# Layer norm, time attention, band attention and feed-forward: scores of two groups in one block, and rstd on other engines

## The chip, the cores and the metric

The kernel runs on one core of a Trainium2 chip. A core has five engines that run at the same time and wait for each other by semaphores: TensorE (PE in the profile; PEld is its weight load), VectorE (DVE), ScalarE (ACT), GpSimd (POOL) and SyncE (SP), which here only issues DMA. Matrix products are written to PSUM, which has 8 banks of 512 float32 values in each of 128 partitions[...]. All data is float32. The metric is the device time in microseconds (us) of one execution.

## The reference, cut to what matters

The input `x` has the shape (B, T, FB, C) = (2, 256, 128, 128). Three residual blocks follow each other: attention over time with a causal mask, attention over bands with a mask of width 16, and a feed-forward block.

```python
def _ln(x, w, b, eps=1e-05):
    mu = x.mean(-1, keepdims=True)
    var = ((x - mu) ** 2).mean(-1, keepdims=True)
    return (x - mu) * jax.lax.rsqrt(var + eps) * w + b

def _mha(x, wi, bi, wo, bo, h, mask):
    c = x.shape[-1]; dh = c // h
    q, k, v = jnp.split(x @ wi.T + bi, 3, axis=-1)
    split = lambda t: t.reshape(t.shape[:-1] + (h, dh)).swapaxes(-2, -3)
    q, k, v = (split(q), split(k), split(v))
    scores = jnp.einsum('...hqd,...hkd->...hqk', q, k) * (1.0 / np.sqrt(dh)) + mask
    o = jnp.einsum('...hqk,...hkd->...hqd', softmax(scores), v)
    return o.swapaxes(-2, -3).reshape(x.shape) @ wo.T + bo

xt = _ln(x, ln_t_w, ln_t_b).transpose(0, 2, 1, 3)
x = x + _mha(xt, t_wi, t_bi, t_wo, t_bo, 4, causal).transpose(0, 2, 1, 3)   # over time, 256 steps
x = x + _mha(_ln(x, ln_f_w, ln_f_b), f_wi, f_bi, f_wo, f_bo, 4, band16)     # over 128 bands
h = gelu(_ln(x, ln_n_w, ln_n_b) @ w1.T + b1)                                # 128 -> 512
x = x + (h @ w2.T + b2)
```

With 256 time steps and tiles of 128 keys, the causal mask leaves, for each head and sequence, the first key tile against both query tiles (256 columns) and the second key tile against the second query tile (128 columns). The two diagonal blocks are cut by a triangle.

## The kernel before, in words

Weights, biases and norm scales are folded beforehand (`fold`). The work is cut into groups of NT = 4 tiles of 128 tokens. First come 128 groups of time attention (`OverTime`; a group is two sequences `s` of 256 steps), which write an intermediate to device memory. Then, for each of 16 runs of 32 time steps, come 8 groups of band attention (`OverBands`) and 8 groups of the feed-forward block (`FeedForward`). I call the first part the time stage.

`BoundedPath.run` is a pipeline written out by hand. One turn of its loop, here called a step, does different stages of several neighbouring groups: scores of group n, the weighted sum of group n - 1, the projections of n + 1, normalizing of n + 3, statistics of n + 4. `do(n, ...)` calls the named stages of a group if it exists, `do_at` only if it is of the named class. All engine instructions go through `InOrder`, so each engine runs them in exactly the order in which the loop calls them; that is why the profile gives the one line 848 (the helper) for nearly all instructions, and why groups are told by tiles. A wait at the head of an engine's queue holds up everything behind it.

The stages of a time group, by the names of their tiles:

- `statistics`: mean and variance (`stats`, then `mv`) by DVE. `root`: rstd = (var + eps) to the power -0.5, by two POOL instructions on 128x4 values (`rstd`).
- `normalize`: four DVE instructions write `xh`. `turn`: DVE transposes 32x32 blocks (`z`) and four DMAs write it to device memory (`turned`). `fetch`: a DMA reads it back transposed (`xnT`).
- `queries_keys`, `values`: products `qp`, `kp`, `vp`, copied by ACT to `qT`, `kT`, `v`. Where the group ahead is attention, `product` splits the weights into four pieces of 32 columns, which stand beside each other in the array.
- scores, `first_half` and `second_half`, one for each sequence: for each of 4 heads a product of 256 columns and one of 128, both with a contraction of 32 rows, so the four heads stand in four row strips of the array. They fill four banks `sp` of 384 columns. ACT takes the exponentials, one instruction a head (`pt<-sp`, 128x384). POOL masks the two diagonal blocks of the four heads (two selects of 128x512), and the sum of the two key tiles' weights for the second queries is formed by POOL for one sequence and by DVE for the other (`pt<-pt`, 128x512).
- `weigh`: weights times values (`op`, contraction of 128, 32 columns a head) and the row sums (`rp`). `invert`: ACT forms 1/rp as exp(-ln(rp)). `divide`: DVE forms `t` and `u` (each with one input in PSUM) and from both `oT`.
- `output`, `finish`: the product `yp`, and DVE adds it to `res`, where POOL (`bias`, `res<-x,orow`) has put x plus a bias row.

PSUM banks come from one pool of 8 buffers, in turn. Lines of code that the change leaves as they are but that matter for it:

```python
vector.scalar_tensor_tensor(self.oT, t, 2.0, u, ALU.subtract, ALU.mult)          # both inputs in SBUF
engine.tensor_tensor(self.block(s, 3), self.block(s, 1), self.block(s, 2), ALU.add)   # both in SBUF
```

Of the kernel before, what the change touches and what calls it, by code (L numbers as in the profile page):

```python
# [19 lines left out]
P = 128  # L20
H = 4
# [414 lines left out]
class Group:  # L436
# [27 lines left out]
    def root(self):  # L464
# [2 lines left out]
        gpsimd.tensor_scalar(self.rstd, self.mv[:, :, 1], EPS, None, ALU.add)  # L467
        gpsimd.tensor_tensor(self.rstd, self.rstd, path.k.mhalf, ALU.pow)

    def normalize(self):  # L470
        path, vector = self.path, self.path.vector
        self.xh = path.work.tile([P, NT, P], F32, name="xh", bufs=2)
        for i in range(NT):
            vector.tensor_scalar(
                self.xh[:, i, :], self.src()[:, i, :], self.mv[:, i, 0:1], self.rstd[:, i : i + 1],
                ALU.subtract, ALU.mult,
            )
# [18 lines left out]
    def first_half(self):  # L496
        pass
# [13 lines left out]
    def second_mask(self):  # L511
        pass

    def last_sum(self):
        pass

    def queries_keys(self):
        pass

# [27 lines left out]

class Attention(Group):
    which = None

    def bias(self):
        self.path.gpsimd.tensor_tensor(
# [3 lines left out]
    def queries_keys(self):  # L556
        path = self.path
        wf = path.k.wf[self.which]
        self.qp = path.bank([P, NT * P], "qp")
        product(path, self.qp, wf[:, 0:P], self.xnT)  # L560

        self.kp = path.bank([P, NT * P], "kp")
        product(path, self.kp, wf[:, P : 2 * P], self.xnT)

    def take_query(self):
# [9 lines left out]
    def values(self):  # L575
        path = self.path
        wv = path.k.wf[self.which][:, 2 * P : 3 * P]
        self.vp = path.bank([P, NT, P], "vp")
        for i in range(NT):
            product(path, self.vp[:, i], self.xnT[:, i * P : (i + 1) * P], wv)  # L580

    def take_values(self):
        path = self.path
        self.v = path.work.tile([P, NT, P], F32, name="v")
        path.scalar.copy(self.v, self.vp)

    def invert(self):
# [27 lines left out]

    def output(self):
        path = self.path
        self.yp = path.bank([P, NT, P], "yp")
        for i in range(NT):
            product(path, self.yp[:, i], self.oT[:, i * P : (i + 1) * P], path.k.wn[self.which])  # L620

# [6 lines left out]
def rows_of(h):  # L628
    return slice(h * D, (h + 1) * D)
# [11 lines left out]
class OverTime(Attention):  # L641

    which = 0
    W = 3 * P

    def scores(self, s):
        path = self.path  # L650
        W, a = self.W, 2 * s * P
        self.sp = [path.bank([P, W], "sp") for h in range(H)]
        for h in range(H):
            r = rows_of(h)
            path.tensor.matmul(
                self.sp[h][:, 0 : 2 * P], self.kT[r, a : a + P], self.qT[r, a : a + 2 * P], start=True, stop=True
            )
        for h in range(H):
            r = rows_of(h)
            path.tensor.matmul(  # L660
                self.sp[h][:, 2 * P : W], self.kT[r, a + P : a + 2 * P], self.qT[r, a + P : a + 2 * P],
                start=True, stop=True,
            )

    def weights(self, s):
        path = self.path
        for h in range(H):
            path.scalar.activation(self.p[:, s, h, 0 : self.W], self.sp[h], AF.Exp)

    def mask(self, s):  # L670
        path = self.path
        for n in (2, 0):
            blk = self.block(s, n)
            path.gpsimd.affine_select(
                out=blk, in_=blk, compare_op=ALU.is_ge, fill=path.zero, base=0,
                pattern=[[0, H], [1, P]], channel_multiplier=-1,
            )

    def block(self, s, n):
        return self.p[:, s, :, n * P : (n + 1) * P]  # L680

    def add(self, engine, s):
        engine.tensor_tensor(self.block(s, 3), self.block(s, 1), self.block(s, 2), ALU.add)

    def first_half(self):
        self.p = self.path.work.tile([P, 2, H, self.W + P], F32, name="pt", tag="p", bufs=2)
        self.scores(0)

    def first_function(self):
        self.weights(0)  # L690

    def first_mask(self):
        self.mask(0)
        self.add(self.path.gpsimd, 0)

    def second_half(self):
        self.scores(1)

    def second_function(self):
        self.weights(1)  # L700

    def second_mask(self):
        self.mask(1)

    def last_sum(self):
        self.add(self.path.vector, 1)

    def weigh_one(self, op, s):
        path, p, v, W = self.path, self.p, self.v, self.W
        for h in range(H):  # L710
            r = rows_of(h)
            path.tensor.matmul(op[r, s, :], v[:, 2 * s, r], p[:, s, h, 0 : 2 * P], start=True, stop=False)
        for h in range(H):
            r = rows_of(h)
            path.tensor.matmul(
                op[r, s, P : 2 * P], v[:, 2 * s + 1, r], p[:, s, h, 2 * P : W], start=False, stop=True
            )

    def weigh(self):
        path = self.path  # L720
        op = path.bank([P, 2, 2 * P], "op")
        rp = path.bank([P, 2, 2 * P], "rp")
        self.weigh_one(op, 0)
        sums = self.p.rearrange("p s h (n q) -> p s h n q", q=P)[:, :, :, 0:4:3, :]
        for h in range(H):
            path.tensor.matmul(rp[rows_of(h), :, :], path.k.ones[:, 0:D], sums[:, :, h], start=True, stop=True)
        self.weigh_one(op, 1)
        self.op = op.rearrange("p s q -> p (s q)")
        self.rp = rp.rearrange("p s q -> p (s q)")


class OverBands(Attention):
# [32 lines left out]
            path.vector.tensor_tensor(blk, blk, path.band.unsqueeze(1).to_broadcast([P, NT, P]), ALU.mult)  # L765

    def first_half(self):
        self.p = self.path.work.tile([P, H, NT, P], F32, name="pf", tag="p", bufs=2)
        self.scores(range(H))

    def weigh(self):
# [15 lines left out]
class FeedForward(Group):  # L787
# [20 lines left out]

    def first_half(self):
        self.hp = {}  # L810
        self.hT = self.path.work.tile([P, self.path.k.NI, NT * P], F32, name="hT")
        self.hidden((0, 1))

    def first_function(self):
# [38 lines left out]
class BoundedPath:  # L853
    def __init__(self, ctx, tc, k):
# [1 line left out]
        self.xpool = ctx.enter_context(tc.tile_pool(name="xpool", bufs=3))  # L856
        self.work = ctx.enter_context(tc.tile_pool(name="work", bufs=3))
        self.small = ctx.enter_context(tc.tile_pool(name="small", bufs=6))
        self.ps = ctx.enter_context(tc.tile_pool(name="ps", bufs=8, space=PSUM))
        self.tensor, self.vector = InOrder(tc, tc.nc.tensor), InOrder(tc, tc.nc.vector)  # L860
        self.scalar, self.gpsimd = InOrder(tc, tc.nc.scalar), InOrder(tc, tc.nc.gpsimd)
        self.dram = ctx.enter_context(tc.tile_pool(name="turns", bufs=3, space=DRAM))
        self.zero = 0.0
        once = ctx.enter_context(tc.tile_pool(name="once", bufs=1))

        self.band = once.tile([P, P], F32, name="band")
        tc.nc.gpsimd.memset(self.band, 1.0)
# [3 lines left out]
                pattern=[[-s, P]], channel_multiplier=s,  # L871
            )

    def bank(self, shape, name):
        return self.ps.tile(shape, F32, name=name, tag="ps")

    @staticmethod
    def of_times(ap, i, f):
# [78 lines left out]
    def run(self, x, out):  # L957
# [17 lines left out]
        for n in range(-11, len(groups) + 2):  # L975
            feeds = [at(n - 2 + i, FeedForward) for i in range(5)]
            bands = [at(n - 2 + i, OverBands) for i in range(5)]
            turn = feeds[2] and bands[1]
            self.by_columns = at(n - 1, Attention)
            do(n + 11, "load")  # L980
            do_at(n + 4, OverTime, "statistics")
            if bands[2] and feeds[1]:
                self.scalar.preload_act_table_set(EXP_SET)
            do(n, "first_half", "first_function", "first_mask")
            if turn:
                do(n, "second_half", "second_function")
            do_at(n + 2, Attention, "fetch")
            do_at(n + 1, FeedForward, "fetch")
            do_at(n + 2, FeedForward, "normalize", "turn")
            do_at(n + 3, Attention, "normalize", "turn")  # L990
            do_at(n + 3, FeedForward, "statistics", "root")
            do_at(n + 4, OverTime, "root")
            if bands[2]:
                do(n, "second_mask")
            do(n - 1, "weigh")
            do(n - 1, "invert_exactly" if turn else "invert")
            if bands[2] or turn:
                do(n - 2, "output", "finish")
            do(n - 1, "divide")
            if not turn:  # L1000
                do(n, "second_half", "second_function")
            if not bands[2]:
                do(n, "second_mask", "bias")
                do_at(n + A, OverBands, "bias")
                if at(n - 1, FeedForward) and at(n - 2, OverBands):
                    do_at(n + A - 1, OverBands, "statistics", "root")
                if not turn:
                    do_at(n + A, OverBands, "statistics", "root")
            do(n + 1, "queries_keys", "take_query", "take_key")
            if not bands[2] and not turn:  # L1010
                do(n - 2, "output", "finish")
            do(n + 1, "values", "take_values")
            do(n, "last_sum")


def bounded_path(tc, k, x, out):
# [66 lines left out]
```

## Time and profile before

| | |
|---|---|
| time, median of 3 | 2792.8 us (2791.96 to 2794.28) |
| busy: PE, DVE, ACT, POOL | 98%, 82%, 65%, 74% of the span |
| time stage | up to about 1030 us |
| DMA | 343.70 MB, mean 123 GB/s |

A row of the timeline gives the start, how long it lasts in us, the engine, the line, the operation, the tiles written and read, the shape and the count of instructions merged into it; in brackets stands how long the engine sat idle before it, and what ended the wait. Matrix products overlap in the array, so the starts of consecutive blocks tell more about what PE needs than their lengths. A row of busy time by windows gives the window, its length, and for PE, PEld, DVE, ACT and POOL the busy us with the number of instructions, then the granted clock of TensorE, the DMA share and the rate.

### The profile page before, as it was taken

How to read it: one execution, taken by the hardware profiler on the slowest of the kernel's cores; microseconds unless marked ns; L12 is line 12 of the kernel's file. 1: busy time of each engine (PE TensorE's matmuls, PEld its weight loads, DVE VectorE, ACT ScalarE, POOL GpSimd, SP SyncE). 2: the span in 40 equal slices, each digit the busy share in tenths (PEclk: the TensorE clock that was granted, in tenths of full speed). 3: DMA queues.
4: the chain of work that ended last, by engine and by line, in shares of the span. 5: the costliest groups of instructions: out<-in, count | busy, mean ns of one | idle time of the engine just before them, and what ended most of it. 6: DMA issues, size and time to landing. Idle time of an engine off the chain costs nothing.

```text
span 2791.8 us, 103916 instructions
## 1 busy us (share of the span) xinstructions
PE 2733.2 (98%) x42534; PEld 1844.4 (66%) x42534; DVE 2302.8 (82%) x6446; ACT 1800.7 (65%) x3328; POOL 2062.7 (74%) x2569
## 2 busy tenths in 40 slices
PE   4999999999999989999999999999999999999998
PEld 3666666666666656676776766767766667667666
DVE  5888888888888899788787797797887887977975
ACT  2888888788888866646546556456466475564563
POOL 3899999999999996666676676676666766766762
PEclk9999999999999999999999999999999999999999
DMA  5555555545555554543544534535435345444333
GB/s 119 134 148 136 139 139 142 145 131 151 133 142 142 140 137 111 131 123 99 140 102 112 132 104 123 129 96 130 127 100 136 104 108 130 103 125 115 83 99 85
DMA packets 471301, 343.70 MB, mean 123 GB/s; under 512 B 43296, under 2 KB 405152, under 8 KB 470816
## 3 DMA queue, kind: packets, MB, share of 16 engines
q1 hardware_dynamic: 469568, 335.92, 46.5%
q8 instruction: 337, 5.52, 0.8%
q14 instruction: 148, 1.21, 0.1%
q10 hardware_dynamic: 1248, 1.05, 0.1%
HBM read 169.03 MB, written 167.77 MB: 121 GB/s over the span
## 4 chain that ended last, share of the span: by engine, by line
PE 89%; DVE 4%; DMA 3%; POOL 3%; SPq 1%; issue 1%; ACT 0%; DVEq 0%; POOLq 0%
PE zp L848 16%; PE hp L848 15%; PE sp L848 12%; PE op L848 9%; PE qp L848 8%; PE rp L848 7%; PE vp L848 7%; PE kp L848 7%; PE yp L848 7%; DMA xnT<-turned 1%; DVE xh L848 1%; POOL pf L848 1%; DMA turned<-z 1%; POOL rstd L848 1%; POOL pt L848 1%
## 5 line engine op out<-in xcount | busy, mean ns | idle before, releaser
L848 POOL TENSOR_SCALAR_AFFINE_SELECT pf<-pf 128x512 f32<-128x512 f32 x768 | 520.9, 694 | 270.6 <-ACT pf L848 244.3
L848 ACT ACTIVATE hT<-hp,b 128x512 f32<-128x512 f32 x512 | 349.3, 687 | 548.6 <-PE hp L848 539.1
L848 DVE TENSOR_SCALAR xh<-x,mv,rstd 128x128 f32<-128x128 f32 x1536 | 624.0, 467 | 17.4 <-POOL rstd L848 17.4
L848 PEld LDWEIGHTS zp<-w2T_sb,hT 128*128 128x128 f32 x4096 | 476.3, 192 | 56.2 <-issue 54.0
L848 PE MATMUL zp<-w2T_sb,hT 128*128 128x128 f32 x4096 | 479.8, 275 | 0.1
L848 PE MATMUL hp<-xnT,w1f 128*128 128x512 f32 x1024 | 470.5, 596 | 6.7 <-DMA xnT<-turned 5.5
L848 POOL TENSOR_TENSOR rstd<-rstd,mhalf 128x4 f32<-128x4 f32 x384 | 446.9, 1164 | 32.0
L848 ACT ACTIVATE pt<-sp 128x384 f32<-128x384 f32 x1024 | 419.5, 497 | 58.8 <-PE sp L848 58.5
L848 PE MATMUL sp<-qT,kT 32*128 32x128 f32 (+1 forms) x8192 | 397.0, 316 | 0.9 <-ACT kT L848 0.8
L848 POOL TENSOR_SCALAR_AFFINE_SELECT pt<-pt 128x512 f32<-128x512 f32 x512 | 323.0, 652 | 79.6 <-ACT pt L848 79.6
L848 PEld LDWEIGHTS sp<-qT,kT 32*128 32x128 f32 x8192 | 315.3, 185 | 83.1 <-issue 31.4
L848 DVE BATCH_NORM_STATS2 stats<-x 128x6 f32<-128x128 f32 x1536 | 326.5, 273 | 7.7 <-DMA x<-in_x 7.7
L848 POOL TENSOR_SCALAR rstd<-mv 128x4 f32<-128x4 f32 x384 | 88.6, 231 | 298.7 <-DVE mv L848 297.5
L848 ACT ACTIVATE pf<-sp 128x512 f32<-128x512 f32 x512 | 264.3, 603 | 62.4 <-PE sp L848 59.1
L848 PEld LDWEIGHTS hp<-xnT,w1f 128*128 128x128 f32 x1024 | 181.1, 190 | 184.6 <-issue 107.9
L848 PE MATMUL qp<-xnT,wf 128*32 128x512 f32 (+1 forms) x1856 | 270.6, 600 | 26.1 <-DMA xnT<-turned 26.1
L848 PEld LDWEIGHTS yp<-wn,oT 128*32 128x32 f32 (+1 forms) x7808 | 234.1, 111 | 83.8 <-issue 61.8
L848 DVE STREAM_TRANSPOSE z<-xh 128x512 f32<-128x512 f32 x384 | 273.2, 712 | 18.8 <-DMA turned<-z 5.7
L848 PEld LDWEIGHTS vp<-wf,xnT 128*32 128x32 f32 (+1 forms) x7424 | 237.3, 113 | 75.0 <-issue 65.5
L848 PE MATMUL vp<-wf,xnT 128*32 128x128 f32 (+1 forms) x7424 | 271.9, 273 | 0.5 <-DVE t L848 0.5
L848 PE MATMUL yp<-wn,oT 128*32 128x128 f32 (+1 forms) x7808 | 271.1, 273 | 0.3 <-DVE t L848 0.3
L848 DVE TENSOR_TENSOR pf<-pf,band 128x512 f32<-128x512 f32 x128 | 117.4, 917 | 184.8 <-ACT pf L848 177.3
(90 smaller groups left out, 3974.0 us busy)
## 6 DMA issues: line engine op xcount, KB each, us to landing
turned<-z SPq DMA_DIRECT2D x1536, 64.0 KB, 2.1
xnT<-turned SPq DMA_DIRECT2D x384, 256.0 KB, 2.7
x<-in_x SPq DMA_DIRECT2D x128, 256.0 KB, 4.6
x<-res SPq DMA_DIRECT2D x256, 128.0 KB, 3.6
x<-x SPq DMA_DIRECT2D x128, 256.0 KB, 4.1
out<-res SPq DMA_DIRECT2D x256, 128.0 KB, 2.6
w1T_sb<-in_w1T ACTq DMA_DIRECT2D x1, 256.0 KB, 3.7
w2T_sb<-in_w2T ACTq DMA_DIRECT2D x1, 256.0 KB, 4.1
```

The source lines that it names most:

```text
L848: return self.tc.keep_in_program_order(emit(*args, **kwargs))
```

## The change

It concerns the time stage above all.

- A step now does the scores of two groups in one block on PE: the second key tile of group n (`old`; 128 columns a head and sequence) and the first key tile of group n + 1 (`new`; 256 columns a head and sequence). The first fill four half banks `b0..b3`, the second four whole banks `a0..a3`. The 16 products are issued in a written order that mixes both kinds over the four row strips.
- ACT takes exponentials of 512 columns (first tiles) and of 256 (second tiles) instead of 384; heads 0 and 3 of the first tiles come later in the step. POOL masks both sequences with one select of 128x1024 for each kind, two a step instead of four.
- The projections, statistics, normalizing and transposes of time groups come one group earlier, and `output` comes before `divide`. The row sums come before the weighted values and in eight products of 256 columns instead of four of 512.
- As the block of scores needs all 8 banks at once, each tile of the time stage gets a bank by name: rp takes that of `b0`, op of `b3`, yp of `a1`, qp of `a2`, kp of `b1`, vp of `b2`, and the roles change from step to step.
- For time groups (and the first band groups) rstd is formed by ACT (Ln, then Exp with scale -0.5) and DVE (three instructions on 128x4 values, one Newton step) instead of by POOL.
- Feed-forward groups do statistics two groups earlier and `root` at the head of a step. Buffers: the weights `p` get 3, `v` 4, and `hT` shares 2 with the second tiles' weights.

```diff
+    def root_by_scalar(self):
+        path, vector = self.path, self.path.vector
+        var = self.mv[:, :, 1]
+        ln = path.small.tile([P, NT], F32, name="lnv")
+        path.scalar.activation(ln, var, AF.Ln, bias=path.eps)
+        y = path.small.tile([P, NT], F32, name="y")
+        path.scalar.activation(y, ln, AF.Exp, scale=-0.5)
+        t = path.small.tile([P, NT], F32, name="vy")
+        vector.scalar_tensor_tensor(t, var, EPS, y, ALU.add, ALU.mult)
+        vector.scalar_tensor_tensor(t, t, -0.5, y, ALU.mult, ALU.mult)
+        self.rstd = path.small.tile([P, NT], F32, name="rstd", bufs=16)
+        vector.scalar_tensor_tensor(self.rstd, t, 1.5, y, ALU.add, ALU.mult)
...
+    def mask(self, blk):
+        path = self.path
+        path.gpsimd.affine_select(
+            out=blk, in_=blk, compare_op=ALU.is_ge, fill=path.zero, base=0,
+            pattern=[[0, 2], [0, H], [1, P]], channel_multiplier=-1,
+        )
...
+def time_scores(old, new):
...
+    for h, second, s in (
+        (0, 1, 0), (1, 0, 0), (2, 0, 0), (3, 1, 0), (0, 1, 1), (3, 1, 1), (0, 0, 0), (3, 0, 0),
+        (1, 0, 1), (2, 0, 1), (0, 0, 1), (3, 0, 1), (1, 1, 0), (2, 1, 0), (1, 1, 1), (2, 1, 1),
+    ):
+        if second and old is not None:
+            old.second_scores(h, s)
+        if not second and new is not None:
+            new.first_scores(h, s)
...
+            old, new = (groups[i] if at(i, OverTime) else None for i in (n, n + 1))
             do(n + 11, "load")
-            do_at(n + 4, OverTime, "statistics")
...
+            do_at(n + 4, FeedForward, "root")
             do(n, "first_half", "first_function", "first_mask")
+            if old is not None or new is not None:
+                time_scores(old, new)
+                b = self.banks
+                Attention.place = dict(rp=b["b0"], op=b["b3"], yp=b["a1"], qp=b["a2"], kp=b["b1"], vp=b["b2"])
...
+            if old is not None:
+                old.second_weights(old.late)
+            if new is not None:
+                new.first_weights(new.early)
+            if old is not None:
+                old.second_weights(old.early)
+                old.mask_second()
...
-            do_at(n + 3, Attention, "normalize", "turn")
-            do_at(n + 3, FeedForward, "statistics", "root")
-            do_at(n + 4, OverTime, "root")
+            do_at(n + 3, OverBands, "normalize", "turn")
+            do_at(n + 4, OverTime, "normalize", "turn")
+            do_at(n + 5, OverTime, "statistics")
...
             do(n - 1, "weigh")
             do(n - 1, "invert_exactly" if turn else "invert")
-            if bands[2] or turn:
+            if new is not None:
+                new.first_weights(new.late)
+                new.mask_first()
+            if old is not None:
+                old.add(self.gpsimd, 0)
+                old.add(self.vector, 1)
+            if bands[2] or turn or old is not None:
                 do(n - 2, "output", "finish")
             do(n - 1, "divide")
+            do_at(n + 5, OverTime, "root_by_scalar")
...
-            do(n + 1, "queries_keys", "take_query", "take_key")
+            do_at(n + 2, OverTime, "queries_keys", "take_query", "take_key")
...
-            do(n, "last_sum")
```

## The prediction

> **What bounds the kernel now.** I read the page first, then the busy time of a quiet stretch of the time stage, then the timeline of one step, then the end of that stage, where the kernel runs differently.
>
> ```profile
> PE 2733.2 (98%) x42534; PEld 1844.4 (66%) x42534; DVE 2302.8 (82%) x6446; ACT 1800.7 (65%) x3328; POOL 2062.7 (74%) x2569
> ...
> 200.00:900.00 700.00, 700.00 (x13936) 440.90 (x13932) 617.17 (x1655) 564.06 (x1195) 645.33 (x735) 1.00 0.54 141
> ```
>
> The columns of the second line are PE, PEld, DVE, ACT, POOL: in these 700 us TensorE never rests, and the others work 88, 81 and 92%. The waits of PE between 60 and 970 us come to 1.5 us. So TensorE paces the quiet time stage. The second part of one step, and the start of the next:
>
> ```profile
> 454.53 0.94 PE L848 MATMUL sp<-qT,kT 32*128 32x256 f32 x16
> 455.39 1.07 PE L848 MATMUL qp<-xnT,wf 128*32 128x512 f32 x8
> 456.28 1.04 PE L848 MATMUL kp<-xnT,wf 128*32 128x512 f32 x8
> 456.63 0.69 DVE L848 SCALAR_TENSOR_TENSOR oT<-t,u 128x512 f32<-128x512 f32 x1
> 456.83 1.39 POOL L848 TENSOR_TENSOR rstd<-rstd,mhalf 128x4 f32<-128x4 f32 x1
> 458.01 1.06 PE L848 MATMUL vp<-wf,xnT 128*32 128x128 f32 x32
> 458.20 1.22 POOL L848 TENSOR_SCALAR_AFFINE_SELECT pt<-pt 128x512 f32<-128x512 f32 x2
> 458.87 1.09 DVE L848 TENSOR_TENSOR pt<-pt 128x512 f32<-128x512 f32 x1
> 458.99 0.94 PE L848 MATMUL sp<-qT,kT 32*128 32x256 f32 x16
> 459.39 1.72 POOL L848 TENSOR_TENSOR res<-x,orow 128x512 f32<-128x512 f32 x1
> ```
>
> The first half of this step's scores started at 451.37, so a step is 458.99 - 451.37 = 7.62 us. Starts tell what a block occupies: kp to the next product 0.85 us for 512 columns; a half of scores, 384 columns, should by that rate take 0.64, yet qp starts 0.86 after sp (+0.22), and sp starts 0.98 after vp (+0.13). Each block of scores costs about 0.35 us beyond its columns, and a step has two.
>
> See also the pair at 458.20 and 458.87. The sum pt on DVE takes 1.09 beside a mask on POOL; a two-input operation of its size, oT, takes 0.69 alone. It ends 0.54 after the mask ends. The other way round, the POOL power behind oT takes 1.39 (1.04 at its shortest). Over the whole trace a two-input DVE operation that starts in the middle of a POOL mask or sum ends 0.54 after that ends, and an xh piece 0.08 after. Now the last eight steps, in which DVE also does statistics and POOL a bias for the band stage:
>
> ```profile
> 985.90 1.28 POOL L848 TENSOR_TENSOR pt<-pt 128x512 f32<-128x512 f32 x1
> 985.97 1.76 DVE L848 SCALAR_TENSOR_TENSOR oT<-t,u 128x512 f32<-128x512 f32 x1
> 987.28 0.94 PE L848 MATMUL sp<-qT,kT 32*128 32x256 f32 x16
> 990.83 1.06 PE L848 MATMUL rp<-pt,ones 128*32 128x512 f32 x8 [1.83 <-DVE pt L848]
> 991.67 2.04 DVE L848 TENSOR_SCALAR xh<-x,mv,rstd 128x128 f32<-128x128 f32 x4
> 996.97 0.94 PE L848 MATMUL sp<-qT,kT 32*128 32x256 f32 x16
> ```
>
> oT waits for all of POOL's sum (1.76), xh takes 2.04 where 1.08 is its shortest, PE waits 1.83 for DVE, and the step is 996.97 - 987.28 = 9.69. DVE's chain has become the bound, and oT and xh alone wait 2.0 us of it for POOL.
>
> **What the Trainium skill says.** "TensorEngine Tiling (Array Packing)", Key Properties: changing the tiling mode drains TensorE. The 0.35 us around each block of scores (row tiles among column tiles) agrees. "SBUF — State Buffer", Who interferes with whom: DVE and GpSimd share a port pair, held exclusively for an instruction; a DVE operation with two SBUF inputs, or in a two-port mode, waits for GpSimd, and the reverse; PSUM inputs do not count. The 1.09, 1.76 and 2.04 above agree, and t and u (one input in PSUM) are never delayed. "ScalarE: Activation LUTs", What ACT_TABLE_LOAD costs: 186 ns + 0.833 ns an element, 93 more for a pointer bias, 93 overlapped; the 384-element exponential here takes 497 ns, 410 each back to back, which agrees.
>
> **The change part by part, per step.**
>
> *One block of scores.* The columns are the same (per head 2x256 + 2x128 = 768, 1.28 us), in one block instead of two: one pair of mode changes goes, -0.335 us after adding both gaps from the raw starts (0.115 + 0.107 + 0.113). PE alone would then need 7.627 - 0.335 = 7.29. The block mixes 128- and 256-column products over the row tiles; the trace shows no such mix. If they don't overlap fully it costs up to 0.21 (one 256-column pass); I take 0, since the listed order would start each product as its row tile comes free.
>
> *Exponentials.* 4x512 + 4x256 instead of 8x384: by the row of pf (516 each back to back) and 410 for 384, the slope is 0.83, so 4x0.516 + 4x0.304 = 3.28, as before (8x0.410). They hide under PE.
>
> *Root.* POOL loses 0.23 + 1.04. ACT gains Ln (pointer bias, 4 elements, about 0.28 less 0.09) and Exp (0.20): ACT, 81% of 7.63 or 6.15 before, + 0.4 = 6.5 of 7.29, hidden. DVE gains three dependent two-input operations on 4 elements: [...]the statistics' aggregate row has 0.14; I take 0.15 each, 0.45 in all (0.10 to 0.18 each).
>
> *Masks.* Two of 1024 instead of four of 512 (0.60 each back to back). POOL's fixed cost is at most the 0.22 of its 4-element operation, so one takes 1.0 to 1.2; I take 1.1. POOL's own work falls to 2x1.1 + 1.26 (sum) + 1.27 (bias, as beside no DVE work) = 4.7, but now in four pieces of over 1 us, three of them back to back: the mask of the first tiles waits for ACT's late exponentials, and the sum and bias queue behind it.
>
> *DVE.* Own work, by start-to-start means: sum 0.65, res 0.66, t 0.58, u 0.67, oT 0.69, xh 4x0.256 = 1.02, z 0.65, bn 0.78, aggregate 0.28 = 6.0, and the new 0.45: 6.45. That is under 7.29 by 0.84, and before it was under 7.63 by 1.63, of which 0.7 went in waits for POOL (88% of 7.63 = 6.7). So the question is whether waits stay under 0.84. Nine DVE pieces now want the port, in the order sum, oT, three roots, four xh, and who comes behind a POOL piece waits for all the rest of it.
>
> A timetable by these durations, times from the start of the scores block. The early exponentials end at 3.1, ln and its Exp at 4.4, the late ones at 5.5. Mask two runs 3.2 to 4.3 (early phase). If PE paced the step, DVE's sum would run 4.4-5.1, and res, t, u to 7.1; oT then meets POOL's sum (6.6-7.9) and ends 8.5; POOL's bias goes next, to 9.6, and the roots behind it wait until then (1.1): waits of 1.9 > 0.84. So DVE slips later each step until it stalls PE. Slipped, the cycle closes like this: the sum is ready at 6.2, waits for mask one (5.54-6.64) and ends 7.18 (+0.3); res to 7.82, t 8.40, u 9.07; oT waits for the bias (8.34-9.61) and ends 10.16 (+0.4); roots to 10.57; three xh to 11.4; the fourth behind the next mask two (11.2-12.38) to 12.47 (+0.8); z, bn, aggregates to 14.13. Then the next sum: 14.13 - 6.20 = 7.93. PE stalls because the next block of scores needs the bank of yp, which res frees at 7.82. What waits on that is all of PE, then ACT and POOL. With masks of 1.0 to 1.25, roots of 0.10 to 0.18 and small shifts of the waits, the same timetable closes between 7.65 and 8.1; middle 7.88.
>
> *Elsewhere.* The last eight steps, four with two sets of statistics at 9.69 and four at 8.33 before (oT's starts are that far apart), become three and five; I cost them at nothing. In the band and feed-forward stages the roots of feed-forward move two steps earlier; PE waits there on the transposed xnT 5.5 us in all, and I take 3 of these back. Buffer counts (hT 3 to 2, p 2 to 3, v 3 to 4) and numbered PSUM banks: readers finish a step earlier, nothing. Fill is one stage deeper but starts its root about 1 us sooner: nothing.
>
> Sum: 120 steady steps x (7.88 - 7.63) = +30; 2792.8 + 30 - 3 = 2820.
>
> **Rivals.**
> - DVE waits stay under 0.84 and PE paces: 7.29 x 120, -40, less 3: 2750. For it: PE is 100% busy now and POOL has less work. Against: the timetable, and the 9.69 us steps, where DVE's own load of 7.1 against 7.63 was already enough to tip over. Without full overlap of the mixed block it is 7.50, or 2775.
> - DVE paces, but its pieces fall luckily into POOL's gaps: 7.63 or a little more, about 2793. For it: DVE waits only 0.7 a step now.
> - Waits pile up as at the end of the stage (oT behind a sum, roots behind the bias, xh behind a mask): 8.2, 120 x 0.57 = +68: 2858.
>
> **Chances.** Forecast 0.60, PE paces 0.15, lucky phases 0.13, piled waits 0.12. Slower: forecast and piled waits and half of the lucky case, 0.78; same 0.05; faster 0.15 + 0.02 = 0.17. The range starts at 2778, leaving out most of the 2750 case, and ends at 2860.
>
> **What would show it.** Right: in a quiet stretch DVE near 100% busy, PE under 97%, sp starting after a wait for DVE res; oT, xh or the roots far over 0.69, 0.31 and 0.15 beside POOL pieces; one sp to qp-like gap fewer. Wrong: PE 100% busy with a step of 7.3, or PE waiting for ACT (kT, or the exponentials) instead of DVE.

## The result, and the profile after

| | before | after |
|---|---|---|
| time, median | 2792.9 us (2791.96 to 2794.28, 4 runs) | 2829.8 us (2828.66 to 2835.57, 4 runs) |
| ratio, 95% interval | | 1.0136 [1.0118, 1.0153] |

The kernel became slower by 37 us; 2820 with a range of 2778 to 2860 had been predicted. The page of after, busy time by engine and the chain that ended last:

```profile
PE 2759.2 (98%) x43522; PEld 1931.2 (68%) x43522; DVE 2347.2 (83%) x6855; ACT 1829.7 (65%) x3600; POOL 1832.7 (65%) x2041
...
PE 85%; DVE 10%; DMA 3%; ACT 1%; issue 1%; SPq 0%; POOL 0%; DVEq 0%
```

POOL lost 230 us of work, and the chain now runs through DVE for 10% of the span (4% before). The quiet stretch of the time stage, in the row of busy time by windows (window, length, PE, PEld, DVE, ACT, POOL, clock, DMA share, GB/s):

```profile
200.00:900.00 700.00, 697.86 (x14324) 483.76 (x14318) 684.47 (x1878) 565.66 (x1342) 460.78 (x358) 1.00 0.54 137
```

DVE went from 617 to 684 of 700 us: 98%, with only short gaps between its instructions. PE's figure hides its stalls: the block of scores shown below counts as busy for 2.12 us, though it stands still for kT within that time. So the step must be taken from starts. From one first row-sum product (rp) to the next it is 7.829 us (mean over steps 20 to 110), against 7.628 before. DVE, POOL, and what concerns PE's block of scores, in one step (mask one is POOL's select on the first key tiles, `mask_first`, here at 508.48; mask two is that on the second, `mask_second`, at 506.36):

```profile
501.49 0.81 DVE L862 TENSOR_TENSOR p<-p,p 128x512 f32<-128x512 f32 x1
501.61 0.30 ACT L862 ACTIVATE lnv<-mv,eps 128x4 f32<-128x4 f32 x1 [1.01 <-DVE mv L862]
501.73 1.72 POOL L862 TENSOR_TENSOR p<-p,p 128x512 f32<-128x512 f32 x1
502.63 0.57 ACT L862 COPY kT<-kp 128x512 f32<-128x512 f32 x1
502.75 2.12 PE L862 MATMUL sp<-qT,kT 32*128 32x128 f32 x32
503.25 1.43 PEld L862 LDWEIGHTS sp<-qT,kT 32*128 32x128 f32 x30 [0.22 <-ACT kT L862]
503.41 1.27 POOL L862 TENSOR_TENSOR res<-x,orow 128x512 f32<-128x512 f32 x1
504.14 1.09 DVE L862 SCALAR_TENSOR_TENSOR oT<-t,u 128x512 f32<-128x512 f32 x1
504.80 1.07 PE L862 MATMUL rp<-p,ones 128*32 128x256 f32 x16
505.15 0.15 DVE L862 SCALAR_TENSOR_TENSOR vy<-mv,y 128x4 f32<-128x4 f32 x1
505.73 1.89 DVE L862 TENSOR_SCALAR xh<-x,mv,rstd 128x128 f32<-128x128 f32 x4
506.36 1.19 POOL L862 TENSOR_SCALAR_AFFINE_SELECT p<-p 128x1024 f32<-128x1024 f32 x1 [1.68 <-ACT p L862]
508.48 1.09 POOL L862 TENSOR_SCALAR_AFFINE_SELECT p<-p 128x1024 f32<-128x1024 f32 x1 [0.93 <-ACT p L862]
```

Three things are to be seen. oT starts in the bias (504.14 against 503.41 to 504.68) and takes 1.09 instead of 0.69: it ends 0.55 after the bias. xh takes 1.89 instead of 1.08, as mask two (506.36) comes upon its pieces. And PE's block starts at 502.75, stops for kT at once, and goes on at 503.25. kT is late because ACT, one place ahead of qT and kT in its queue, sat 1.01 us waiting for mv. Block to rp lasts 2.05 us; where nothing stops it, 1.52 (third experiment). The waits in the window, summed (us, times, longest):

```profile
ACT lnv L862 <- DVE mv L862: 89.9, 89, 1.2
```

DVE's slip is thus passed to PE by ACT's queue.

Where the added time lies, by the starts of rp and of the first feed-forward product hp (the profiled runs, spans 2791.8 and 2827.6):

| stretch | before | after | difference |
|---|---|---|---|
| start to the first rp | 55.1 | 58.0 | +2.9 |
| 119 middle steps | 908.9 | 932.0 | +23.1 |
| the last eight steps | 71.1 | 82.6 | +11.5 |
| to the first hp | 48.7 | 50.5 | +1.8 |
| band and feed-forward stages | 1708.0 | 1704.5 | -3.5 |

The first of the last eight steps takes 15.24 us:

```profile
996.42 1.27 POOL L862 TENSOR_TENSOR res<-x,orow 128x512 f32<-128x512 f32 x1
997.64 1.73 POOL L862 TENSOR_TENSOR x<-x,orow 128x512 f32<-128x512 f32 x1
998.16 1.24 DVE L862 SCALAR_TENSOR_TENSOR vy<-mv,y 128x4 f32<-128x4 f32 x1
999.34 1.09 POOL L862 TENSOR_SCALAR_AFFINE_SELECT p<-p 128x1024 f32<-128x1024 f32 x1
999.43 1.01 DVE L862 SCALAR_TENSOR_TENSOR vy<-vy,y 128x4 f32<-128x4 f32 x1
1001.45 1.09 POOL L862 TENSOR_SCALAR_AFFINE_SELECT p<-p 128x1024 f32<-128x1024 f32 x1 [1.03 <-DVE stats L862]
1001.62 4.70 DVE L862 TENSOR_SCALAR xh<-x,mv,rstd 128x128 f32<-128x128 f32 x4
1002.51 1.28 POOL L862 TENSOR_TENSOR p<-p,p 128x512 f32<-128x512 f32 x1
1003.75 1.26 POOL L862 TENSOR_TENSOR res<-x,orow 128x512 f32<-128x512 f32 x1
1004.97 1.26 POOL L862 TENSOR_TENSOR x<-x,orow 128x512 f32<-128x512 f32 x1
1008.13 0.30 ACT L862 ACTIVATE lnv<-mv,eps 128x4 f32<-128x4 f32 x1 [6.74 <-DVE mv L862]
1010.19 2.94 PE L862 MATMUL sp<-qT,kT 32*128 32x256 f32 x30 [6.12 <-ACT kT L862]
```

Two operations on 128x4 values, 0.15 and 0.16 alone, take 1.24 and 1.01 because each waits out a POOL instruction (it ends within 0.02 us of that one's end); the four pieces of xh take 4.70 behind mask, sum and two biases. mv comes behind them, lnv waits 6.74 for it, and PE 6.12 for kT behind lnv.

### The profile page after: what moved, and what is told of

Same layout as the page of the kernel before. It is cut to its first block, busy times and chain, and to the rows that moved or that the text cites. A ratio compares the mean times of both kernels' runs of the same rounds, so it can differ in the third digit from the quotient of the medians.

```text
span 2827.6 us, 106284 instructions
## 1 busy us (share of the span) xinstructions
PE 2759.2 (98%) x43522; PEld 1931.2 (68%) x43522; DVE 2347.2 (83%) x6855; ACT 1829.7 (65%) x3600; POOL 1832.7 (65%) x2041
## 3 DMA queue, kind: packets, MB, share of 16 engines
q14 instruction: 150, 1.23, 0.2%
q10 hardware_dynamic: 1248, 1.05, 0.1%
## 4 chain that ended last, share of the span: by engine, by line
PE 85%; DVE 10%; DMA 3%; ACT 1%; issue 1%; SPq 0%; POOL 0%; DVEq 0%
PE zp L862 16%; PE hp L862 16%; PE sp L862 12%; PE op L862 8%; PE rp L862 7%; PE vp L862 6%; PE qp L862 6%; PE kp L862 6%; PE yp L862 6%; DVE xh L862 3%; DVE oT L862 1%; DMA x<-in_x 1%; DVE stats L862 1%; DVE z L862 1%; DMA turned<-z 1%; DVE vy L862 1%
## 5 line engine op out<-in xcount | busy, mean ns | idle before, releaser
L862 POOL TENSOR_SCALAR_AFFINE_SELECT pf<-pf 128x512 f32<-128x512 f32 x768 | 544.6, 722 | 181.7 <-ACT pf L862 155.5
L862 DVE TENSOR_SCALAR xh<-x,mv,rstd 128x128 f32<-128x128 f32 x1536 | 569.5, 433 | 4.5
L862 POOL TENSOR_SCALAR_AFFINE_SELECT p<-p 128x1024 f32<-128x1024 f32 x256 | 287.6, 1124 | 381.4 <-ACT p L862 337.4
L862 ACT ACTIVATE p<-sp 128x512 f32<-128x512 f32 (+1 forms) x1024 | 417.1, 500 | 67.9 <-PE sp L862 67.4
L862 PE MATMUL sp<-qT,kT 32*128 32x128 f32 (+1 forms) x8192 | 433.4, 314 | 23.8 <-DVE u L862 8.7
L862 PEld LDWEIGHTS sp<-qT,kT 32*128 32x128 f32 x8192 | 359.3, 186 | 96.3 <-ACT kT L862 53.5
L862 POOL TENSOR_SCALAR rstd<-mv 128x4 f32<-128x4 f32 x248 | 56.6, 228 | 355.5 <-DVE mv L862 355.1
L862 DVE TENSOR_TENSOR res<-zp,res 128x512 f32<-128x512 f32 x128 | 87.7, 685 | 235.0 <-PE zp L862 234.9
L862 POOL TENSOR_TENSOR rstd<-rstd,mhalf 128x4 f32<-128x4 f32 x248 | 256.6, 1035 | 20.7
L862 PE MATMUL kp<-xnT,wf 128*32 128x512 f32 (+1 forms) x1850 | 266.9, 593 | 0.0
```

The source lines that it names most:

```text
L862: return self.tc.keep_in_program_order(emit(*args, **kwargs))
```

## The experiments

All times and ratios stand against runs of before on the same chip (medians 2791.5 to 2793.3); a comparison with after is across chips, between which before itself differs by 1.8 us. Theory A of the runs is the prediction's: DVE paces the step, by its own work and its waits behind POOL's pieces.

**1. The root calls behind kT in ACT's queue.** Both root_by_scalar calls of after move:

```diff
-            do_at(n + 5, OverTime, "root_by_scalar")
...
             do_at(n + 2, OverTime, "queries_keys", "take_query", "take_key")
             do_at(n + 1, OverBands, "queries_keys", "take_query", "take_key")
+            do_at(n + 5, OverTime, "root_by_scalar")
```

> The changed kernel with the rstd of time groups (Ln, Exp, and the three DVE pieces) called after the copy of kT instead of before qT, so that nothing of the projections stands behind Ln in ACT's queue; DVE's and POOL's orders stay. Theory A (DVE's own chain with its waits of 1.3 us a step for POOL sets the pace): still 7.8 us a step, 2800 to 2840 us, DVE still 98% busy. Theory B (Ln waits 1.0 us a step for mv at the head of ACT's queue and holds up qT, kT and so the next scores): the wait is gone, 7.3 us a step, about 2768 us.

2802.7 us, ratio 1.0035 [1.0020, 1.0049], 27 us less than after. lnv's wait is gone, but the step is 7.669, far from theory B's 7.3, and DVE is as full as in after:

```profile
200.00:900.00 700.00, 700.00 (x14624) 496.49 (x14616) 684.09 (x1916) 587.40 (x1369) 472.39 (x366) 1.00 0.54 140
```

PE's block now waits for u, whose bank it takes over (in one step its last products begin at 504.47, when u ends; sp to rp 1.91). The last eight steps take 73.5 instead of 82.6, though the small pieces keep their place in DVE's queue. So ACT's queue was one way in which DVE's lateness reached PE: without it most of the loss against before is gone, 0.16 us a step and 9.1 us at the end of the stage. Still DVE paces, 0.38 us a step above the 7.29 that PE needs.

**2. rstd without its Newton step.** After with `rstd = exp(-0.5 ln(var + eps))` straight from ACT; the three DVE pieces, and with them the Newton correction of rstd, are left out:

```diff
-        t = path.small.tile([P, NT], F32, name="vy")
-        vector.scalar_tensor_tensor(t, var, EPS, y, ALU.add, ALU.mult)
-        vector.scalar_tensor_tensor(t, t, -0.5, y, ALU.mult, ALU.mult)
...
-        vector.scalar_tensor_tensor(self.rstd, t, 1.5, y, ALU.add, ALU.mult)
+        self.rstd = y
```

> The changed kernel with the Newton step left out: rstd is ACT's exp(-0.5 ln(var + eps)) itself, so DVE loses three pieces of 0.15 to 0.16 us a step (0.475) and three claims on the shared port. Theory A: DVE needs 6.0 of its own and at most the 1.3 of waits it has now, 7.3 us, where TensorE is the bound at 7.29: about 2765 to 2775 us. Theory B: the Ln stays where it is and still waits for mv, 2800 to 2830 us. Theory C (DVE is too long by what it does itself, waits or not): 0.475 x 120 = 57 less, 2773 us, which does not tell it from A.

2747.2 us, 0.9840 [0.9823, 0.9856], 18 us below the range of theory A. The step is 7.287 and PE is busy 700.00 of 700:

```profile
200.00:900.00 700.00, 700.00 (x15380) 487.18 (x15372) 693.35 (x1732) 628.22 (x1442) 491.23 (x384) 1.00 0.57 147
```

With 0.475 us a step less of DVE's own work PE paces again. DVE's waits did not shrink (table below). What the expectation left out is the end of the stage: the last eight steps take 65.5 instead of 82.6.

**3. POOL's sum ahead of mask one.** No work is added or taken away:

```diff
             if new is not None:
                 new.first_weights(new.late)
-                new.mask_first()
             if old is not None:
                 old.add(self.gpsimd, 0)
                 old.add(self.vector, 1)
+            if new is not None:
+                new.mask_first()
```

> The changed kernel with one exchange in POOL's queue: the sum of the old group goes before the mask of the new group's first tiles, instead of behind it. Every instruction, and the orders of PE, ACT and DVE, stay as they are. Theory A: POOL's sum and bias no longer stand where DVE's oT, roots and xh come, the waits fall under the slack of 0.84 us, and TensorE paces at 7.3: about 2768 us. Theory B and theory C: no difference, 2820 to 2840 us.

2763.2 us, 0.9897 [0.9880, 0.9913]: 67 us less than after, by two instructions changing places in one queue. The step is 7.287, PE 700.00 of 700. DVE and POOL in one step:

```profile
501.52 1.12 DVE L862 TENSOR_SCALAR xh<-x,mv,rstd 128x128 f32<-128x128 f32 x4
502.55 1.09 POOL L862 TENSOR_SCALAR_AFFINE_SELECT p<-p 128x1024 f32<-128x1024 f32 x1 [2.09 <-ACT p L862]
503.73 1.28 POOL L862 TENSOR_TENSOR p<-p,p 128x512 f32<-128x512 f32 x1
504.34 1.22 DVE L862 TENSOR_TENSOR p<-p,p 128x512 f32<-128x512 f32 x1
504.96 1.55 POOL L862 TENSOR_SCALAR_AFFINE_SELECT p<-p 128x1024 f32<-128x1024 f32 x1
506.49 1.27 POOL L862 TENSOR_TENSOR res<-x,orow 128x512 f32<-128x512 f32 x1
507.39 0.92 DVE L862 SCALAR_TENSOR_TENSOR oT<-t,u 128x512 f32<-128x512 f32 x1
```

In after POOL idles twice a step, 1.68 ahead of mask two and 0.93 ahead of mask one, and its row of sum and bias comes late. Here the sum runs where POOL would have waited for the late exponentials, POOL's pieces close up, and its idle time lies in one gap of 2.09, in which the xh pieces run almost undisturbed (1.12). DVE's sum now waits 0.57 instead, less than is saved.

**4. The root part alone.** Before, with root_by_scalar for the time groups:

```diff
-            do_at(n + 4, OverTime, "root")
...
             do(n - 1, "divide")
+            do_at(n + 4, OverTime, "root_by_scalar")
```

> The kernel before with the rstd of time groups alone changed to ACT and DVE (scores as before; small buffers cut to fit). Theory A: DVE has 6.0 + 0.45 of its own and some 0.7 of waits against 7.63, still under it: 2793 within 6 us, TensorE paces. If the root had a cost of its own at any place: 0.45 x 120 = 54 more, 2847 us.

2961.8 us, 1.0610 [1.0592, 1.0628]: slower by 170 us, which no theory had expected. The step is 9.04. Part of one:

```profile
500.92 1.11 DVE L862 SCALAR_TENSOR_TENSOR oT<-t,u 128x512 f32<-128x512 f32 x1
501.45 1.71 POOL L862 TENSOR_TENSOR res<-x,orow 128x512 f32<-128x512 f32 x1
501.95 1.23 DVE L862 SCALAR_TENSOR_TENSOR vy<-mv,y 128x4 f32<-128x4 f32 x1
504.92 1.07 PE L862 MATMUL rp<-pt,ones 128*32 128x512 f32 x8 [0.98 <-DVE pt L862]
505.76 2.25 DVE L862 TENSOR_SCALAR xh<-x,mv,rstd 128x128 f32<-128x128 f32 x4
```

oT, the first root piece and xh all wait for POOL, 2.7 us a step in all.

**5. The scores part alone.** After, with POOL's root for the time groups and the first band groups, at the same place:

```diff
-            do_at(n + 5, OverTime, "root_by_scalar")
+            do_at(n + 5, OverTime, "root")
             if at(n - 1, OverTime):
-                do_at(n + A - 1, OverBands, "root_by_scalar")
+                do_at(n + A - 1, OverBands, "root")
```

> After with the inverse root of the time groups (and of the last band groups) given back to GpSimd's power: the scores part of the change alone. Theory A (the three small pieces on VectorE and the waits behind GpSimd's shared port set after's 7.83 us step; the scores part is a gain by itself): VectorE falls to about 6.0 us of own work and some 1.3 us of waits, GpSimd holds 5.2 us of masks, sums and residuals and 1.6 us of root, both below 7.3, so TensorE paces at 7.29: 2745 to 2765 us. Theory C (the large masks beside VectorE's pieces cost the time whoever makes rstd): the step stays near 7.8 and the time near 2825.

2867.6 us, 1.0267 [1.0250, 1.0284]. Neither theory: no engine is full (PE 652, DVE 641 of 700), and steps of 7.29 and 9.1 us alternate. The waits between 200 and 900 us:

```profile
DVE xh L862 <- POOL rstd L862: 53.7, 43, 1.2
...
PE sp L862 <- DVE res L862: 47.6, 43, 1.2
```

In every second step POOL's power, in its queue behind masks and sum, is late for xh, and what DVE loses there PE loses on res. DVE's work and its waits for POOL come to 7.5 us a step as well (table below), above what PE needs even without the wait for rstd.

**6. The root part alone, without the Newton step.** Experiment 4 with rstd as ACT's Exp leaves it (the Newton correction is left out):

```diff
-        path.scalar.activation(y, ln, AF.Exp, scale=-0.5)
...
+        path.scalar.activation(self.rstd, ln, AF.Exp, scale=-0.5)
```

> Before with rstd of the time groups as exp(-0.5 ln(var + eps)) on ScalarE only: the fourth experiment without its three small VectorE pieces (so without the Newton correction of rstd). Theory A (the three pieces and their waits made 2793 into 2962): TensorE paces again at 7.62 us a step, 2785 to 2795 us. Rival (the move of the root to ScalarE hurts by itself: lnv waits for mv at the head of ScalarE's queue and holds the exponentials and kT): a step over 8 us, 2840 or more.

2833.6 us, 1.0138 [1.0121, 1.0155], at 8.09 us a step. The three pieces made 128 of experiment 4's 170 us, but 40 remain though DVE has no more work of its own than before, and POOL 1.3 us less. Theory A as worded fell here too. The step of over 8 us is what its rival (ScalarE) had said; experiment 12 tries that rival.

**7. The band groups' root by POOL.** After, only in the last eight steps:

```diff
             if at(n - 1, OverTime):
-                do_at(n + A - 1, OverBands, "root_by_scalar")
+                do_at(n + A - 1, OverBands, "root")
```

> After with the inverse root of only the first eight band groups (made in the last eight time steps) given back to GpSimd; the time groups keep theirs. The 120 middle steps stay at 7.83. Theory D (the small pieces of the band groups, each let in only between two GpSimd instructions, make the last eight steps 11.5 us longer than before's): the last eight steps fall from 82.6 to about 75 us, the time to about 2822. Theory E (the four xh pieces wait there behind the unbroken row of mask, sum, residual and bias whoever makes rstd): the last eight steps stay over 81 us, and the time within 3 us of 2830.

2820.3 us, 1.0097 [1.0080, 1.0114]. The middle step is 7.830 as in after; the last eight steps take 70.6 instead of 82.6, about as long as before's 71.1, and the whole kernel 9.5 us less. Theory D holds against E. But the pieces are not the whole cause: in experiment 1 they stay, and with lnv moved behind kT these steps take 73.5. The pieces and lnv's place in ACT's queue make this loss together, and taking either away gives most of it back. What the same place looks like here:

```profile
1001.65 2.77 DVE L862 TENSOR_SCALAR xh<-x,mv,rstd 128x128 f32<-128x128 f32 x4
1002.55 1.27 POOL L862 TENSOR_TENSOR p<-p,p 128x512 f32<-128x512 f32 x1
1003.79 0.23 POOL L862 TENSOR_SCALAR rstd<-mv 128x4 f32<-128x4 f32 x1
1004.11 1.05 POOL L862 TENSOR_TENSOR rstd<-rstd,mhalf 128x4 f32<-128x4 f32 x1
1005.13 1.26 POOL L862 TENSOR_TENSOR res<-x,orow 128x512 f32<-128x512 f32 x1
```

xh takes 2.77 instead of 4.70. Its first two pieces wait out mask one (not shown) and the sum; the last two need not wait for the two biases, as POOL's root stands in between, 1.3 us in which DVE isn't held.

**8. Experiments 2 and 3 together** (no Newton correction, sum ahead of mask one).

> After with both gains: GpSimd's sum ahead of mask one, and rstd without its Newton pieces. Theory A: TensorE already paces at 7.29 us a step with either alone, so the middle gains nothing more; the last eight steps and the ramp are those of the second experiment at best: 2740 to 2750 us, within 0.2% of the second experiment. Rival (the waits of VectorE still push single steps over 7.29): more than 5 us below the second experiment.

2747.4 us, 0.9833 [0.9816, 0.9849], the same as experiment 2. At 7.287 us a step PE is the floor.

**9. The scores part alone in the better order:** experiment 5 with the edit of experiment 3.

> The scores part alone (rstd by GpSimd's power, as in the fifth experiment), with GpSimd's sum ahead of mask one. Theory F (the fifth experiment's 7.29/9.1 us pattern came from where the instructions stand in GpSimd's queue: the power stood behind two masks and the sum, and xh waited 1.25 us for it in every second step): with the sum out of the way of mask one and the xh pieces no longer behind two masks in a row, xh meets its rstd in most steps; TensorE paces at 7.29 to 7.45 us, 2755 to 2785 us. Theory G (the power, 1.04 us a step, has no room in GpSimd's queue of this step, wherever the sum stands): the step stays over 8 us, 2840 or more.

2784.7 us, 0.9973 [0.9964, 0.9982], at the edge of F's range: most steps are 7.29, about every fourth 8.16, and xh no longer waits for rstd. The mean of 7.50 is above F's 7.45; DVE is busy 694 of 700, so it is probably what makes the odd long step; no run shows this apart.

**10. Experiments 3 and 7 together.**

> After with GpSimd's sum ahead of mask one (third experiment) and the first eight band groups' inverse root by GpSimd's power (seventh experiment). If the two losses are separate, one in the 120 middle steps and one in the last eight, they add: 2763 - 9.5 = 2753.7 us, within 4 us. If the swapped order had already taken the last steps' waits, it gains under 3 us over the third experiment: over 2760.

2755.5 us, 0.9869 [0.9853, 0.9886]. That is within the 4 us of the expected sum, but the two gains are not wholly separate. The middle steps are 7.287, as with the exchange alone. Of the last eight steps' 82.6 us the exchange alone takes 5.8 (76.8), POOL's root alone 12.0, and both together 11.5 (71.1). This is the fastest version that keeps all of after's arithmetic for the time groups, 37 us below before and 74 below after.

**11. No mask one.** After with its line `new.mask_first()` left out, so the diagonal blocks of the first key tiles keep their weights above the diagonal.

> After without mask one of the time groups (the diagonal blocks of the first key tiles keep their weights above the diagonal): 1.09 us a step of GpSimd's work taken away, and nothing of VectorE's, ScalarE's or TensorE's. Theory A (VectorE's xh pieces lose 0.9 us a step behind GpSimd's two masks in a row): that wait falls below 0.4 us, VectorE drops under 7.2 us a step, TensorE paces at 7.29, 2755 to 2770 us. Rival (VectorE's own 6.45 us and the queues' order set the 7.83 us step, GpSimd's hold of the port is not the cause): the step stays within 0.1 us of 7.83 and the time within 10 us of 2830.

2757.2 us, 0.9875 [0.9858, 0.9891], 7.289 us a step, as theory A expected:

```profile
502.25 0.69 DVE L862 SCALAR_TENSOR_TENSOR oT<-t,u 128x512 f32<-128x512 f32 x1
503.45 1.12 DVE L862 TENSOR_SCALAR xh<-x,mv,rstd 128x128 f32<-128x128 f32 x4
504.72 1.09 POOL L862 TENSOR_SCALAR_AFFINE_SELECT p<-p 128x1024 f32<-128x1024 f32 x1 [3.16 <-ACT p L862]
```

xh falls to 1.12 and oT to 0.69 though no operation of DVE's was touched: both now lie in the 3.16 us in which POOL is idle ahead of mask two. The expectation speaks of two masks in a row, but in after xh meets mask two alone. By these timelines mask one acts from afar: it pushes sum and bias back to where oT comes.

**12. A root that nobody reads.** Experiment 6 with POOL's two root instructions kept where before has them, into a spare tile: pure added work.

```diff
+    def root_unused(self):
+        path, gpsimd = self.path, self.path.gpsimd
+        spare = path.small.tile([P, NT], F32, name="spare", bufs=2)
+        gpsimd.tensor_scalar(spare, self.mv[:, :, 1], EPS, None, ALU.add)
+        gpsimd.tensor_tensor(spare, spare, path.k.mhalf, ALU.pow)
...
+            do_at(n + 4, OverTime, "root_unused")
```

> The sixth experiment (before, with the time groups' rstd by ScalarE's ln and exp and no Newton pieces: 2834 us, 8.09 us a step) with GpSimd's own root kept where before has it, written to a tile that nobody reads. Only work is added: 1.3 us a step on GpSimd. Theory H (the power, which doesn't hold the shared port, held GpSimd's residual and masks back into a place where VectorE doesn't want the port; without it they meet oT, xh and the sum for 1.9 us a step): the step returns to 7.63 to 7.70 us, 2788 to 2802 us, faster than the sixth experiment by over 30 us. Rival (ScalarE's ln and exp are what slows the sixth experiment, by the later exponentials): the added work changes nothing or makes it worse, 2830 us or more.

2792.0 us, 1.0001 [0.9992, 1.0009], 7.627 us a step: 42 us faster than experiment 6 by doing more. First a step of experiment 6, then one of this:

```profile
546.32 1.67 POOL L857 TENSOR_SCALAR_AFFINE_SELECT pt<-pt 128x512 f32<-128x512 f32 x2 [0.73 <-ACT pt L857]
546.36 1.13 DVE L857 SCALAR_TENSOR_TENSOR oT<-t,u 128x512 f32<-128x512 f32 x1
```

```profile
501.79 1.04 POOL L863 TENSOR_TENSOR spare<-spare,mhalf 128x4 f32<-128x4 f32 x1
502.29 0.69 DVE L863 SCALAR_TENSOR_TENSOR oT<-t,u 128x512 f32<-128x512 f32 x1
502.80 1.27 POOL L863 TENSOR_SCALAR_AFFINE_SELECT pt<-pt 128x512 f32<-128x512 f32 x2
505.60 1.08 DVE L863 TENSOR_SCALAR xh<-x,mv,rstd 128x128 f32<-128x128 f32 x4
```

POOL's power stands beside oT and doesn't hold it up, keeps the masks back until oT is nearly through, and the row behind it leaves xh free too (in this step; in the mean xh takes 1.44, against 2.04 in experiment 6). In the step shown the power starts first, as in 22 steps of this run. In 96 others oT starts first and the power waits for it, taking 1.5 instead of 1.04, so that the masks come behind oT there too. oT takes 0.69 in both cases. So theory H holds in what it says of the order, but "doesn't hold the port" is only half of it: the power holds up nothing, yet it is held up. ACT's ln and exp cost nothing here.

What ties the runs together, in us a step between 200 and 900 us. "Waits" is what the sum, oT, the four xh and the root pieces take beyond 0.66, 0.69, 1.08 and 0.15 to 0.16; "rest" is DVE's busy time less that.

| kernel | step | DVE busy | sum | oT | xh | waits | rest |
|---|---|---|---|---|---|---|---|
| before | 7.63 | 6.73 | 1.04 | 0.69 | 1.43 | 0.7 | 6.0 |
| after | 7.83 | 7.66 | 0.81 | 1.09 | 1.90 | 1.4 | 6.3 |
| 1 root behind kT | 7.67 | 7.49 | 0.66 | 1.09 | 1.89 | 1.2 | 6.3 |
| 2 no Newton | 7.29 | 7.22 | 0.66 | 1.11 | 2.06 | 1.4 | 5.8 |
| 3 sum first | 7.29 | 7.11 | 1.23 | 0.91 | 1.12 | 0.8 | 6.3 |
| 4 root alone | 9.04 | 8.91 | 0.68 | 1.05 | 2.23 | 2.7 | 6.2 |
| 5 scores alone | 8.20 | 7.50 | 1.05 | 1.05 | 1.98 | 1.7 | 5.8 |
| 6 the same as 4, no Newton | 8.09 | 7.78 | 1.38 | 0.93 | 2.04 | 1.9 | 5.9 |
| 9 scores alone, sum first | 7.50 | 7.43 | 1.20 | 0.82 | 2.04 | 1.6 | 5.8 |
| 11 no mask one | 7.29 | 7.12 | 1.45 | 0.69 | 1.12 | 0.8 | 6.3 |
| 12 root twice | 7.63 | 6.72 | 1.04 | 0.69 | 1.44 | 0.7 | 6.0 |

The rest depends on whether DVE does the three root pieces (6.2 to 6.3 with them, 5.8 to 6.0 without), and on hardly anything else. The waits run from 0.7 to 2.7; a change of order alone takes them from 1.4 to 0.8 (after and 3), and work added to POOL from 1.9 to 0.7 (6 and 12). Where rest, waits and the short gaps exceed what PE needs (7.63 in the kernels made from before, 7.29 in those from after), the step is longer than that. In experiment 5 a wait for rstd comes on top.

## Why the prediction was right, and where not

- *TensorE alone 7.29.* Right: five kernels (experiments 2, 3, 8, 10, 11) run at 7.287 to 7.289 with PE full. This also settles the cost of the mixed block, taken as 0 with a bound of 0.21: from its start to rp it takes 1.52, where 1.28 for its columns and the gap of 0.22 make 1.50. Making one block of two was worth 7.627 - 7.287 = 0.34 us, as the gaps of before had shown (0.335). "TensorEngine Tiling (Array Packing)", Key Properties, says that changing the tiling mode drains TensorE; no run here shows that this drain is what fills the gaps.
- *DVE paces, through waits that exceed 0.84.* Right in kind and size: experiments 2, 3 and 11 took away, each by another means, DVE's own work or its waits for POOL, and PE paced in each. Predicted waits 0.3 + 0.4 + 0.8 for the sum, oT and the fourth xh; measured 0.15, 0.40 and 0.82. The root pieces took 0.475 in all against 0.45, a mask 1.09 against 1.1. The timetable as written closed at 7.93, and 7.88 was the middle of its range; the trace has 7.83: +23 for +30. The rule behind it, of "SBUF — State Buffer", Who interferes with whom, agrees for masks, sums and biases: oT ended 0.55 us after the bias that it met. It does not fit POOL's power: by the page the engine that comes second is blocked for the whole instruction of the other, and oT beside the power took 0.69 (experiment 12).
- *PE waits for yp's bank, freed by res.* Wrong: PE waited for kT, behind ACT's wait for mv, one of the signs that the prediction had listed against itself. It costed ACT's ln and exp as work (0.4, hidden), and left out that the first of them waits for DVE at the head of a queue in which kT stands. It also expected PE's busy share under 97%, and the row of after's quiet stretch shows 99.7% (697.86 of 700), as stalls within the block count as busy. The cost is not small: with the wait moved away (experiment 1) the kernel is 27 us faster, 0.16 a step and 9.1 in the last eight steps. But DVE still paces then, so this link passed DVE's lateness on and did not make it.
- *The last eight steps cost nothing.* Wrong, the largest miss: +11.5. Before's 9.69 us steps were read, but the small pieces were not put into them. There POOL's pieces stand without a gap, and each small DVE piece gets in only after the one that it meets; then mv, lnv and kT come late behind it. Either end of this chain can be cut: experiment 7 takes 12.0 us off these steps by taking the band groups' pieces away, experiment 1 takes 9.1 by moving lnv behind kT.
- *Feed-forward -3, fill nothing.* -3.5 and +2.9, with +1.8 between the stages. The sum is 23.1 + 11.5 + 2.9 + 1.8 - 3.5 = 35.8 of span against +27. That the total comes within 10 us of the forecast owes something to luck: the middle was put 7 too high, everything else but feed-forward 16 too low, and the range from 2778 to 2860 was wide enough to hold before's own 2793.
- *Which half of the change is to blame?* The prediction priced POOL's root as 1.27 us of relieved work. Experiments 4, 6 and 12 show that in the kernel before it was also a spacer: its removal costs 40 us of itself (42 when it is put back unused), 170 with the three pieces. But the scores part alone, in after's order, is slower too (experiment 5). So neither half is a gain as placed; with POOL's sum moved, the scores part is a gain of 7 us with POOL's root (experiment 9) and the whole change one of 28 (experiment 3). My expectations for experiments 4, 5 and 6 failed by the same error: they added up work and took waits as fixed.

Left open is why the waits settle at a given value in each order. The timelines show which pieces meet, and the runs that order decides it; no rule was found that gives 9.04 for experiment 4 in advance. Whether POOL's root at another place in its queue would serve the scores part better than in experiment 9 was not tried.

## What to carry to other kernels

When two engines share a port, count the idle time of one as a resource of the other and ask where it lies: 2.6 us of POOL idle time in two pieces left xh 0.8 us of waiting, and 2.1 in one piece under the xh none to speak of. Before work is moved off an engine that is not the bottleneck, look at what then moves up in its queue and whom that meets; and look at the stretch where the same row stands without gaps, as a tiny operation costs a whole neighbour there. And when a change loses, try the orders of its instructions before giving up its parts: here one such change of places was worth 67 us, where 37 had been lost.

## What the hardware did that I had not expected

- A DVE operation of 128x4 values takes 0.15 us alone and 1.23 or 1.24 when it meets a POOL instruction of 128x512 (experiment 4 and the 15.24 us step of after); its size is no help.
- Between two POOL instructions that follow each other at once, one DVE piece got in: the four xh pieces of the 15.24 us step took 4.70 us beside a row of four POOL instructions, and each ended about 0.08 us after one of them.
- POOL's power on 128x4 values takes 1.04 us, and an oT that starts in the midst of it takes 0.69, as alone. Not all busy time on POOL is thus time in which DVE is held up. The other way round the power does wait: it takes 1.5 where oT started first (experiment 12).
